# First expert weights as the stationary operand, loaded tile by tile from DRAM

## The chip, the cores and the metric

The kernel runs on one core of a Trainium2 chip. Times are device microseconds of one launch. Three runs of the kernel before took 886.35, 894.93 and 897.02 us; their median, 894.93, is the time before. The profile is of a further execution, of 883.17 us, whose span from the first to the last instruction is 881.4 us.

## The reference

`x` has 16 x 256 tokens of 128 numbers. The network adds a mixture of experts, an attention and the same mixture again:

```python
x = x + 0.5 * _L0_ffn_ref(_layernorm(x), ...)
x = x + _L0_attn_ref(_layernorm(x), ...)
x = x + 0.5 * _L0_ffn_ref(_layernorm(x), ...)
```

In the mixture each token goes to 4 of 32 experts:

```python
t = _rmsnorm(x, norm_scale)
g = t @ gate_w.T + gate_b
vals, idx = jax.lax.top_k(gf, K)
w = jax.nn.softmax(vals, axis=-1)
h1 = jnp.einsum('th,efh->tef', tf, w1) + b1
h = _swiglu(h1)          # min(glu, 7) * sigmoid(1.702 * glu) * (clip(lin, -7, 7) + 1)
hw = h * combine[:, :, None]
out = jnp.einsum('tef,ehf->th', hw, w2) + combine @ b2
return x + out
```

The reference computes all experts and weights most with zero; the kernel computes the chosen ones only. All numbers are float32.

## The kernel before

**Groups and runs.** The 4096 tokens are two groups of four blocks of 512 tokens. Each group passes the mixture twice, so there are four expert runs, called f0, f1 (first mixture, group 0 and 1) and l0, l1 (second mixture). In names of tiles the page shows `_f` for f0 and f1, `_l` for l0 and l1. `route` chooses the experts of a block; `dispatch` sorts the rows of a group by expert, makes the table `at_w` (which expert each tile of rows belongs to) and scatters the rows into the DRAM buffer `xs` with indirect DMAs from POOL. `experts` computes one run and writes its rows into the DRAM buffer `ys`. `combined` gathers them back (`gt`), weights and adds them (`pu`).

**A quad.** Rows come in tiles of 125 rows of one expert; four tiles are a quad, and a run has 28 quads. For quad q, `experts` calls three functions:

- `enter` loads the quad's rows `xq` from `xs` (two DMAs on SP, L658), transposes the four tiles on PE into `pxT` (L650), and copies that on ACT to `xT` (L652).
- `first` reads the four experts from `at_w` into PE's registers (L631), multiplies each tile of `xT`, which is the stationary operand, by 256 columns of its expert's weights in `w_sb` (L671: `ph`, two tiles to a PSUM tile), and forms the gated product `a`: Silu on ACT (L675), clipping into `lin` on DVE (L676), both for two tiles at a time, and one scalar_tensor_tensor on DVE for all four (L681, called STT in what follows). Tokens lie on the partitions.
- `second` transposes `a` on PE into `phT` (L650), copies that on ACT to `hT` (L652), multiplies by the second weights, also in `w_sb` (L688: `po`), copies `po` to `yq` on ACT (L693) and writes `yq` to `ys` (two DMAs on SP, L695).

The loop calls `enter(q + 1)`, `first(q)` and `second(q - 1)`, and then `beside()`, which advances the background work of another group by a few steps:

```python
beside = [enter(1), middle(0), middle(1), leave(0)]
steps = [2, 5, 5, 2]
```

So f0 has the routing of group 1 beside it, f1 and l0 have combination, attention and routing of a group, and l1 has the last combination of group 0. `leave(1)` follows alone.

**Order.** The program is recorded in this order and a scheduler then places each engine's instructions in one order of that engine, by its own estimate of when they can run. On the chip an engine follows its list. SP's list holds all DMAs but the indirect ones; a DMA there also waits until the DMA eight places earlier on the list has landed, since eight semaphores are used in turn.

**Weights.** `w_sb` holds for each of the 32 experts 256 columns of first weights and 128 of second weights, loaded at the start. `fold_experts` multiplies the norm's scale and the first bias into the first weights in place: for every two experts two matmuls (L285, L286: `pw`) and one DVE instruction (L289). Attention's weights are folded in `fold_attention`. `xs` is cleared at the start by DMAs from a tile of zeros.

Of the kernel before, what the change touches and what calls it, by code (L numbers as in the profile page):

```python
# [10 lines left out]
F32 = mybir.dt.float32  # L11
# [3 lines left out]
AF = mybir.ActivationFunctionType  # L15
ALU = mybir.AluOpType
AX = mybir.AxisListType
PE = mybir.EngineType.PE
DVE = mybir.EngineType.DVE
PSUM = bass.MemoryType.PSUM  # L20
DRAM = bass.MemoryType.DRAM

P = 128
NJ = 4
# [4 lines left out]
NE = 32  # L29
# [1 line left out]
NH = 16  # L31
HD = 8
KVW = P + NH
EW = 3 * P


RB = 5
# [3 lines left out]
RT = BT * RB  # L41
# [5 lines left out]
LIMIT = 7.0  # L47
ALPHA = 1.702
# [7 lines left out]
def kernel(  # L56
# [22 lines left out]
    nc = tc.nc  # L79
# [9 lines left out]
    wpool = ctx.enter_context(tc.tile_pool(name="weights", bufs=1))  # L89
# [151 lines left out]
        )  # L241


    w_sb = wpool.tile([P, NE, EW], F32, tag="w_sb", name="w_sb")
    for c in range(NE // 8):
        s = slice(c * 8, (c + 1) * 8)
        nc.sync.dma_start(w_sb[:, s, 0 : 2 * P], w1[:, s].rearrange("h e t f -> h e (t f)"))
        nc.sync.dma_start(w_sb[:, s, 2 * P : EW], w2[:, s])
    w_flat = w_sb.rearrange("p e c -> p (e c)")

    cleared(0)

# [60 lines left out]
    pairs = []  # L313
# [8 lines left out]
        pairs.append(pr)  # L322

    def fold_experts():
        for c in range(NE // 2):
            folded(
                w_sb[:, 2 * c : 2 * c + 2, 0 : 2 * P], b1_w.rearrange("p r f -> p (r f)"),
                pairs[c // (NE // 4)][:, c % (NE // 4), :], f"w{c}",
            )
        nc.vector.tensor_scalar(b2_sb, b2_sb, ALPHA, None, ALU.mult)  # L330

# [176 lines left out]
    def dispatch(st):  # L508

        name, n = st.name, st.n  # L510
# [51 lines left out]
        st.at_w = small.tile([P, NT], I32, tag="at_w", name=f"at_w_{name}")  # L562
        ex = small.tile([P, NT], F32, tag="ex", name=f"ex_{name}")
        nc.vector.tensor_scalar(ex, pex[:, 0:NT], float(NE - 1), None, ALU.min)
        nc.vector.tensor_scalar(st.at_w, ex, float(EW), None, ALU.mult)
        yield
        sc = []
        for b in range(GB):
# [58 lines left out]
                yield  # L627
        scattered[name] = sc

    def loaded(tab, q, engine, top):  # L630
        _, vals = nc.values_load_multi_w_load_instructions(  # L631
            tab[0:1, q * NJ : (q + 1) * NJ], engines=[engine],
            min_val=0, max_val=top, skip_runtime_bounds_check_because="made on the chip from at most NE - 1",
        )
        return vals

    def experts(st, beside):
# [4 lines left out]
        xT, hw, off = {}, {}, {}  # L642

        parts = slice(0, RT // 16 * 16), slice(RT // 16 * 16, RT)

        def turned(src, name):

            pt = ps_t.tile([P, NJ, P], F32, tag="tp", name=f"p{name}")
            for t in range(NJ):
                nc.tensor.transpose(pt[:, t, 0:RT], src[:, t, :], ident[:RT, :RT])  # L650
            dst = ep.tile([P, NJ, RT], F32, tag=name[0:2], name=name)
            nc.scalar.copy(dst, pt[:, :, 0:RT])  # L652
            return dst

        def enter(q):
            xq = ep.tile([RT, NJ, P], F32, tag="xq", name=f"xq_{name}_{q}", bufs=2)
            for rows in parts:
                nc.sync.dma_start(xq[rows], xs_q[q].rearrange("j m h -> m j h")[rows])  # L658
            xT[q] = turned(xq, f"xT_{name}_{q}")

        def first(q):
            off[q] = loaded(st.at_w, q, PE, (NE - 1) * EW)
            a = ep.tile([RT, NJ, P], F32, tag="a", name=f"a_{name}_{q}")
            lin = ep.tile([RT, NJ, P], F32, tag="lin", name=f"lin_{name}_{q}")
            x_q = xT.pop(q)
            for c in range(2):
                ph = ps_h.tile([P, 2, 2 * P], F32, tag="ph", name=f"ph_{name}_{q}_{c}")
                ts = slice(2 * c, 2 * c + 2)
                for s in range(2):
                    t = 2 * c + s  # L670
                    nc.tensor.matmul(  # L671
                        ph[:RT, s, :], x_q[:, t, :],
                        w_flat[:, bass.ds(off[q][t], 2 * P)], start=True, stop=True,
                    )
                nc.scalar.activation(a[:, ts, :], ph[:RT, :, 0:P], AF.Silu, scale=ALPHA)  # L675
                nc.vector.tensor_scalar(  # L676
                    lin[:, ts, :], ph[:RT, :, P : 2 * P], LIMIT + 1.0, 1.0 - LIMIT,
                    ALU.min, ALU.max,
                )

            nc.vector.scalar_tensor_tensor(a, a, SILU_LIMIT, lin, ALU.min, ALU.mult)  # L681
            hw[q] = a

        def second(q):
            hT = turned(hw.pop(q), f"hT_{name}_{q}")
            po = ps_o.tile([P, NJ, P], F32, tag="po", name=f"po_{name}_{q}")
            for t in range(NJ):
                nc.tensor.matmul(  # L688
                    po[:RT, t, :], hT[:, t, :],
                    w_flat[:, bass.ds(off[q][t] + 2 * P, P)], start=True, stop=True,  # L690
                )
            yq = ep.tile([RT, NJ, P], F32, tag="yq", name=f"yq_{name}_{q}", bufs=2)
            nc.scalar.copy(yq, po[:RT])  # L693
            for rows in parts:
                nc.sync.dma_start(ys_q[q].rearrange("j m h -> m j h")[rows], yq[rows])  # L695
# [296 lines left out]
```

## Time and profile before

| | |
|---|---|
| median of three runs | 894.93 us (886.35 to 897.02) |
| profiled execution | 883.17 us, span 881.4 us |
| granted TensorE clock, mean | 0.967 |
| busy: PE, DVE, ACT, POOL | 87%, 61%, 55%, 18% of the span |
| DMA moved | 134.22 MB, mean 152 GB/s |
| HBM read, written | 62.88 MB, 70.27 MB |

A line of the timeline has the start, the length, the engine, the line of the kernel, the operation and its tiles (out<-in), and in square brackets the idle time before it and what ended it. A PE record of a float32 matmul comes twice, since it is made in two passes; a transpose comes once. A record's length reaches past the start of the next, since PE is a pipeline; so spacing of starts, and not length, tells what one costs. `x8` joins eight neighbours. `SPq` is SP's queue. A line of a group has busy time, mean length of one in ns, idle time of the engine before them and what ended it.

### The profile page before, as it was taken

What the parts mean: (1) busy time and instruction counts of PE and PEld (TensorE: products, weight loads), DVE (VectorE), ACT (ScalarE), POOL (GpSimd) and SP (SyncE); (2) the same over time, 40 slices, a digit from 0 to 9 for tenths busy, and PEclk for the clock granted to TensorE, in tenths of its full rate; (3) what the DMA queues carried; (4) which work ended last, traced back from release to release, by engine and by line L of the source; (5) the groups of instructions that cost most, each with busy time, mean ns of one, the idle gap of its engine ahead of it and who ended that gap; (6) DMA issues with size and microseconds to landing.
All of it is one profiled execution on the core that took longest, in us unless ns stands there. A gap on an engine that the chain in (4) does not pass through costs nothing.

```text
span 881.4 us, 16078 instructions
## 1 busy us (share of the span) xinstructions
PE 766.5 (87%) x5018; PEld 648.3 (74%) x5033; DVE 538.3 (61%) x1903; ACT 486.6 (55%) x964; POOL 155.6 (18%) x211
## 2 busy tenths in 40 slices
PE   4789689899979898989998989888898899999566
PEld 2336578799868787877887878777797788787456
DVE  6676875675554876758854777676874344433232
ACT  1412288755556588697453687968655345455100
POOL 4003400022212201000434112000242321000232
PEclk9999989999999999999999999999999999999688
DMA  8996535455545434224556344223465665553442
GB/s 259 342 355 238 178 116 156 110 161 176 181 135 148 139 92 138 70 71 135 172 179 180 100 136 132 81 83 87 150 201 163 181 175 160 140 143 93 116 133 84
DMA packets 155505, 134.22 MB, mean 152 GB/s; under 512 B 10528, under 2 KB 143136, under 8 KB 155424
## 3 DMA queue, kind: packets, MB, share of 16 engines
q1 hardware_dynamic: 145184, 91.24, 36.3%
q0 software_dynamic: 10240, 41.95, 14.7%
q8 instruction: 44, 0.72, 0.3%
q14 instruction: 37, 0.30, 0.1%
HBM read 62.88 MB, written 70.27 MB: 151 GB/s over the span
## 4 chain that ended last, share of the span: by engine, by line
PE 56%; ACT 12%; DVE 6%; DMA 5%; issue 4%; POOL 1%; SPq 0%; POOLq 0%; ACTq 0%; DVEq 0%
PE ph_l L671 9%; PE ph_f L671 8%; PE po_l L688 6%; PE po_f L688 5%; PE pu_l L749 4%; PE pu_f L749 4%; PE p_l L610 3%; ACT hT_l L652 2%; PE phT_l L650 2%; PE phT_f L650 2%; ACT L675 2%; ACT hT_f L652 2%; PE p_f L610 2%; PE pxT_f L650 1%; PE pxT_l L650 1%
## 5 line engine op out<-in xcount | busy, mean ns | idle before, releaser
L671 PE MATMUL ph_f<-w_sb,xT_f 128*125 x448 | 114.4, 388 | 3.6 <-DVE lin_f L676 2.9
L671 PE MATMUL ph_l<-w_sb,xT_l 128*125 x448 | 111.2, 383 | 0.9 <-PE pq L270 0.3
L676 DVE TENSOR_SCALAR lin_l<-ph_l 125x256 f32<-125x256 f32 x112 | 46.1, 421 | 85.9 <-ACT a_l L675 85.6
L671 PEld LDWEIGHTS ph_f<-w_sb,xT_f 128*125 128x125 f32 x448 | 78.4, 190 | 15.1 <-DVE lin_f L676 3.6
L671 PEld LDWEIGHTS ph_l<-w_sb,xT_l 128*125 128x125 f32 x448 | 78.1, 187 | 13.8 <-issue 3.2
L676 DVE TENSOR_SCALAR lin_f<-ph_f 125x256 f32<-125x256 f32 x112 | 45.7, 420 | 53.9 <-ACT a_f L675 53.7
L688 PE MATMUL po_f<-w_sb,hT_f 128*125 x448 | 64.1, 286 | 12.9 <-ACT hT_f L652 12.2
L688 PE MATMUL po_l<-w_sb,hT_l 128*125 x448 | 64.3, 287 | 11.9 <-ACT hT_l L652 11.1
L688 PEld LDWEIGHTS po_l<-w_sb,hT_l 128*125 128x125 f32 x448 | 54.5, 190 | 23.0 <-ACT hT_l L652 21.8
L688 PEld LDWEIGHTS po_f<-w_sb,hT_f 128*125 128x125 f32 x448 | 54.4, 190 | 22.8 <-ACT hT_f L652 21.6
L749 PE MATMUL pu_l<-gt_l,u_l 128*128 128x128 f32 x320 | 52.5, 311 | 16.2 <-DMA gt_l<-ys,row_l 12.1
L749 PEld LDWEIGHTS pu_l<-gt_l,u_l 128*128 128x128 f32 x320 | 48.6, 225 | 20.6 <-issue 14.8
L693 ACT COPY yq_l<-po_l 125x512 f32<-125x512 f32 x56 | 32.8, 586 | 55.4 <-PE po_l L688 50.0
L675 ACT ACTIVATE a_l<-ph_l 125x256 f32<-125x256 f32 x112 | 42.0, 385 | 35.8 <-PE ph_l L671 35.1
L693 ACT COPY yq_f<-po_f 125x512 f32<-125x512 f32 x56 | 32.7, 585 | 47.5 <-PE po_f L688 39.7
L719 POOL DMA_INDIRECT gt_f<-ys,row_f x32 | 31.6, 986 | 151.2 <-PE pu_f L749 94.3
L675 ACT ACTIVATE a_f<-ph_f 125x256 f32<-125x256 f32 x112 | 41.4, 384 | 29.8 <-PE ph_f L671 29.0
L719 POOL DMA_INDIRECT gt_l<-ys,row_l x32 | 31.0, 970 | 144.4 <-PE pu_l L749 63.4
L675 ACT ACT_TABLE_LOAD x41 | 52.6, 1283 | 2.8 <-PE ph_l L671 1.0
L749 PE MATMUL pu_f<-gt_f,u_f 128*128 128x128 f32 x320 | 45.8, 287 | 5.7 <-DMA gt_f<-ys,row_f 5.7
L616 POOL DMA_INDIRECT xs<-s_l,row_l x32 | 33.5, 1046 | 92.1 <-ACT s_l L614 61.9
L616 POOL DMA_INDIRECT xs<-s_f,row_f x32 | 31.8, 994 | 90.2 <-DVE o_f L602 69.2
(325 smaller groups left out, 1702.5 us busy)
## 6 DMA issues: line engine op xcount, KB each, us to landing
xs<-zero SPq DMA_DIRECT2D x2, 7000.0 KB
xq_f<-xs SPq DMA_DIRECT2D x56, 224.0 KB
ys<-yq_f SPq DMA_DIRECT2D x56, 224.0 KB
xq_l<-xs SPq DMA_DIRECT2D x56, 224.0 KB
ys<-yq_l SPq DMA_DIRECT2D x56, 224.0 KB
w_sb<-in_w_dram SPq DMA_DIRECT2D x4, 1024.0 KB
x<-in_x_dram SPq DMA_DIRECT2D x8, 256.0 KB
w_sb<-in_w_dram SPq DMA_DIRECT2D x4, 512.0 KB
```

Source lines behind the costliest of these rows:

```text
L610: nc.tensor.matmul(p0[:, r, :] if r < 4 else p1[:, 0:P], o[:, r, :], k.tn[:, t, :], start=True, stop=True,)
L616: ins = nc.gpsimd.indirect_dma_start(out=xs[st.g][:, :], out_offset=bass.IndirectOffsetOnAxis(ap=st.row[:, 1, j : j + 1], axis=0), in_=s.r ...
L650: nc.tensor.transpose(pt[:, t, 0:RT], src[:, t, :], ident[:RT, :RT])
L652: nc.scalar.copy(dst, pt[:, :, 0:RT])
L671: nc.tensor.matmul(ph[:RT, s, :], x_q[:, t, :], w_flat[:, bass.ds(off[q][t], 2 * P)], start=True, stop=True,)
L675: nc.scalar.activation(a[:, ts, :], ph[:RT, :, 0:P], AF.Silu, scale=ALPHA)
L676: nc.vector.tensor_scalar(lin[:, ts, :], ph[:RT, :, P : 2 * P], LIMIT + 1.0, 1.0 - LIMIT, ALU.min, ALU.max,)
L688: nc.tensor.matmul(po[:RT, t, :], hT[:, t, :], w_flat[:, bass.ds(off[q][t] + 2 * P, P)], start=True, stop=True,)
L693: nc.scalar.copy(yq, po[:RT])
L719: nc.gpsimd.indirect_dma_start(out=gt.rearrange("p r h -> p (r h)"), out_offset=None, in_=ys[st.g][:, :], in_offset=bass.IndirectOffsetOnA ...
L749: nc.tensor.matmul(pu[:, t, :], u[:, r, s, :], got[t][:, r, :], start=(r == 0), stop=False)
```

## The change

The first matmul's operands change places: the weights of 128 columns are stationary and the 125 rows of `xT` stream, so `ph` comes out with the hidden index on the partitions, and the gated product can be the second matmul's stationary operand as it is. The second transposition and its copy are gone. There are twice as many first matmuls, of 125 columns each.

The first weights no longer stay in SBUF. After the fold they are written to a DRAM buffer `w1_d`, and `enter` loads for each tile its expert's 128 x 256 weights from there, four DMAs a quad on SP whose DRAM address comes from a register; SP reads `at_w` for that itself. The tiles are six buffers deep. The same six buffers serve the fold: six of its eight parts of four experts are loaded at the start, and parts 6 and 7 take over a buffer once part 0 and part 1 have been written to `w1_d`. The second weights stay in SBUF, in `w2_sb`, and PE reads `at_w` in `second`.

```diff
-    w_sb = wpool.tile([P, NE, EW], F32, tag="w_sb", name="w_sb")
+    WE = 4
+    w1_d = dram.tile([NE, P, 2 * P], F32, tag="w1_d", name="w1_d")
+    w1_rows = w1_d.rearrange("e h c -> (e h) c")
+    w2_sb = wpool.tile([P, NE, P], F32, tag="w2_sb", name="w2_sb")
+    w2_flat = w2_sb.rearrange("p e c -> p (e c)")
+
+    def w1_tile(name):
+        return ep.tile([P, WE, 2 * P], F32, tag="w1", name=name, bufs=6)
+
+    w1_parts = {}
+
+    def load_w1(c):
+        w1_parts[c] = w1_tile(f"w1_{c}")
+        s = slice(c * WE, (c + 1) * WE)
+        nc.sync.dma_start(w1_parts[c], w1[:, s].rearrange("h e t f -> h e (t f)"))
+
+    for c in range(6):
+        load_w1(c)
     for c in range(NE // 8):
         s = slice(c * 8, (c + 1) * 8)
-        nc.sync.dma_start(w_sb[:, s, 0 : 2 * P], w1[:, s].rearrange("h e t f -> h e (t f)"))
-        nc.sync.dma_start(w_sb[:, s, 2 * P : EW], w2[:, s])
-    w_flat = w_sb.rearrange("p e c -> p (e c)")
+        nc.sync.dma_start(w2_sb[:, s], w2[:, s])
...
     def fold_experts():
-        for c in range(NE // 2):
-            folded(
-                w_sb[:, 2 * c : 2 * c + 2, 0 : 2 * P], b1_w.rearrange("p r f -> p (r f)"),
-                pairs[c // (NE // 4)][:, c % (NE // 4), :], f"w{c}",
+        for c in range(NE // WE):
+            if c not in w1_parts:
+                load_w1(c)
+            part = w1_parts.pop(c)
+            for i in range(WE // 2):
+                d = c * WE // 2 + i
+                folded(
+                    part[:, 2 * i : 2 * i + 2, :], b1_w.rearrange("p r f -> p (r f)"),
+                    pairs[d // (NE // 4)][:, d % (NE // 4), :], f"w{d}",
+                )
+            nc.sync.dma_start(
+                w1_d[c * WE : (c + 1) * WE].rearrange("e h c -> h e c"), part
             )
...
-        def turned(src, name):
-
-            pt = ps_t.tile([P, NJ, P], F32, tag="tp", name=f"p{name}")
-            for t in range(NJ):
-                nc.tensor.transpose(pt[:, t, 0:RT], src[:, t, :], ident[:RT, :RT])
-            dst = ep.tile([P, NJ, RT], F32, tag=name[0:2], name=name)
-            nc.scalar.copy(dst, pt[:, :, 0:RT])
-            return dst
...
         def enter(q):
             xq = ep.tile([RT, NJ, P], F32, tag="xq", name=f"xq_{name}_{q}", bufs=2)
             for rows in parts:
                 nc.sync.dma_start(xq[rows], xs_q[q].rearrange("j m h -> m j h")[rows])
-            xT[q] = turned(xq, f"xT_{name}_{q}")
+            w1_q[q] = w1_tile(f"w1_{name}_{q}")
+            at = loaded(st.at_w, q, SP)
+            for t in range(NJ):
+                nc.sync.dma_start(w1_q[q][:, t, :], w1_rows[bass.ds(at[t], P), :])
+            pt = ps_t.tile([P, NJ, P], F32, tag="tp", name=f"pxT_{name}_{q}")
+            for t in range(NJ):
+                nc.tensor.transpose(pt[:, t, 0:RT], xq[:, t, :], ident[:RT, :RT])
+            xT[q] = ep.tile([P, NJ, RT], F32, tag="xT", name=f"xT_{name}_{q}")
+            nc.scalar.copy(xT[q], pt[:, :, 0:RT])
 
         def first(q):
-            off[q] = loaded(st.at_w, q, PE, (NE - 1) * EW)
-            a = ep.tile([RT, NJ, P], F32, tag="a", name=f"a_{name}_{q}")
-            lin = ep.tile([RT, NJ, P], F32, tag="lin", name=f"lin_{name}_{q}")
-            x_q = xT.pop(q)
+
+            a = ep.tile([P, NJ, RT], F32, tag="a", name=f"a_{name}_{q}")
+            lin = ep.tile([P, NJ, RT], F32, tag="lin", name=f"lin_{name}_{q}")
+            x_q, w_q = xT.pop(q), w1_q.pop(q)
             for c in range(2):
-                ph = ps_h.tile([P, 2, 2 * P], F32, tag="ph", name=f"ph_{name}_{q}_{c}")
+                ph = ps_h.tile([P, 2, 2, P], F32, tag="ph", name=f"ph_{name}_{q}_{c}")
                 ts = slice(2 * c, 2 * c + 2)
                 for s in range(2):
                     t = 2 * c + s
-                    nc.tensor.matmul(
-                        ph[:RT, s, :], x_q[:, t, :],
-                        w_flat[:, bass.ds(off[q][t], 2 * P)], start=True, stop=True,
-                    )
-                nc.scalar.activation(a[:, ts, :], ph[:RT, :, 0:P], AF.Silu, scale=ALPHA)
+                    for part in range(2):
+                        nc.tensor.matmul(
+                            ph[:, part, s, 0:RT], w_q[:, t, part * P : (part + 1) * P],
+                            x_q[:, t, :], start=True, stop=True,
+                        )
+                nc.scalar.activation(a[:, ts, :], ph[:, 0, :, 0:RT], AF.Silu, scale=ALPHA)
                 nc.vector.tensor_scalar(
-                    lin[:, ts, :], ph[:RT, :, P : 2 * P], LIMIT + 1.0, 1.0 - LIMIT,
+                    lin[:, ts, :], ph[:, 1, :, 0:RT], LIMIT + 1.0, 1.0 - LIMIT,
                     ALU.min, ALU.max,
                 )
...
         def second(q):
-            hT = turned(hw.pop(q), f"hT_{name}_{q}")
+            at = loaded(st.at_w, q, PE)
+            hT = hw.pop(q)
             po = ps_o.tile([P, NJ, P], F32, tag="po", name=f"po_{name}_{q}")
             for t in range(NJ):
                 nc.tensor.matmul(
-                    po[:RT, t, :], hT[:, t, :],
-                    w_flat[:, bass.ds(off[q][t] + 2 * P, P)], start=True, stop=True,
+                    po[:RT, t, :], hT[:, t, :], w2_flat[:, bass.ds(at[t], P)],
+                    start=True, stop=True,
                 )
```

More of the change, by code (lines that the diff above doesn't have):

```diff
@@ L18 @@
 PE = mybir.EngineType.PE
-DVE = mybir.EngineType.DVE
+SP = mybir.EngineType.SP
 PSUM = bass.MemoryType.PSUM
@@ L33 @@
 KVW = P + NH
-EW = 3 * P
 RB = 5
@@ L564, in dispatch @@
         nc.vector.tensor_scalar(ex, pex[:, 0:NT], float(NE - 1), None, ALU.min)
-        nc.vector.tensor_scalar(st.at_w, ex, float(EW), None, ALU.mult)
+        nc.vector.tensor_scalar(st.at_w, ex, float(P), None, ALU.mult)
         yield
@@ L628, in dispatch, with loaded @@
         scattered[name] = sc
-    def loaded(tab, q, engine, top):
+    def loaded(tab, q, engine):
         _, vals = nc.values_load_multi_w_load_instructions(
             tab[0:1, q * NJ : (q + 1) * NJ], engines=[engine],
-            min_val=0, max_val=top, skip_runtime_bounds_check_because="made on the chip from at most NE - 1",
+            min_val=0, max_val=(NE - 1) * P, skip_runtime_bounds_check_because="made on the chip from at most NE - 1",
         )
@@ L641, in experts @@
         ys_q = ys[g].rearrange("(q j n) (r h) -> q j (n r) h", j=NJ, n=BT, r=RB)
-        xT, hw, off = {}, {}, {}
+        xT, w1_q, hw = {}, {}, {}
         parts = slice(0, RT // 16 * 16), slice(RT // 16 * 16, RT)
-        def turned(src, name):
-            pt = ps_t.tile([P, NJ, P], F32, tag="tp", name=f"p{name}")
-            for t in range(NJ):
-                nc.tensor.transpose(pt[:, t, 0:RT], src[:, t, :], ident[:RT, :RT])
-            dst = ep.tile([P, NJ, RT], F32, tag=name[0:2], name=name)
-            nc.scalar.copy(dst, pt[:, :, 0:RT])
-            return dst
         def enter(q):
```

## The prediction, on record before the changed kernel ran

> **What bounds the kernel.** I read the page's engine shares first, then the chain that ended last, then the four expert runs as windows, then one quad in the timeline.
>
> ```profile
> PE 766.5 (87%) x5018; PEld 648.3 (74%) x5033; DVE 538.3 (61%) x1903; ACT 486.6 (55%) x964; POOL 155.6 (18%) x211
> ...
> PE 56%; ACT 12%; DVE 6%; DMA 5%; issue 4%; POOL 1%; SPq 0%; POOLq 0%; ACTq 0%; DVEq 0%
> ```
>
> PE is busiest and holds most of the chain. The windows run from the first yq copy of a run to its last (f0, f1, l0, l1); columns are length, busy time of PE, PEld, DVE, ACT, POOL, clock, DMA share, GB/s.
>
> ```profile
> 124.70:255.30 130.60, 121.58 (x875) 108.49 (x875) 79.14 (x256) 87.09 (x177) 15.96 (x19) 1.00 0.51 149
> 269.40:466.00 196.60, 178.93 (x1273) 156.73 (x1276) 139.99 (x503) 139.83 (x276) 31.24 (x35) 0.99 0.43 125
> 479.80:675.70 195.90, 178.48 (x1271) 156.85 (x1274) 140.02 (x503) 139.72 (x275) 30.79 (x32) 0.99 0.43 126
> 686.50:820.50 134.00, 124.77 (x830) 108.52 (x833) 56.97 (x124) 66.54 (x136) 16.13 (x16) 1.00 0.54 143
> ```
>
> The four make 657 of 881.4 us and PE is busy 91 to 93% of each, so experts are bound by what PE does and waits for. The shortest quad, in l1 with no background work beside it:
>
> ```profile
> 788.26 1.14 PE L688 MATMUL po_l<-w_sb,hT_l 128*125 x8 [0.29 <-ACT hT_l L652]
> ...
> 789.24 1.92 PE L671 MATMUL ph_l<-w_sb,xT_l 128*125 x8
> ...
> 790.09 0.82 SPq L695 DMA_DIRECT2D ys<-yq_l  x2
> ...
> 790.99 0.59 PE L650 MATMUL phT_l<-ident,a_l 125*128 125x125 f32 x4
> 791.19 0.39 ACT L675 ACTIVATE a_l<-ph_l 125x256 f32<-125x256 f32 x1 [0.43 <-PE ph_l L671]
> ...
> 791.42 0.59 PE L650 MATMUL pxT_l<-ident,xq_l 125*128 125x125 f32 x4
> 791.61 0.42 DVE L676 TENSOR_SCALAR lin_l<-ph_l 125x256 f32<-125x256 f32 x1 [0.39 <-ACT a_l L675]
> 791.67 0.58 ACT L652 COPY hT_l<-phT_l 128x500 f32<-128x500 f32 x1
> 792.04 0.81 SPq L658 DMA_DIRECT2D xq_l<-xs  x2
> 792.07 0.69 DVE L681 SCALAR_TENSOR_TENSOR a_l<-a_l,lin_l 125x512 f32<-125x512 f32 x1
> 792.14 0.58 ACT L652 COPY xT_l<-pxT_l 128x500 f32<-128x500 f32 x1
> 792.30 1.14 PE L688 MATMUL po_l<-w_sb,hT_l 128*125 x8 [0.30 <-ACT hT_l L652]
> ```
>
> A quad takes 792.30 - 788.26 = 4.04 us. Starts of neighbouring records lie 216 ns apart for 256 moving columns, 109 for 128, 106 for the transposes' 125. PE work: pxT 4 x 0.106, ph 8 x 0.216, phT 4 x 0.106, po 8 x 0.109, in all 3.45. The rest is the wait for hT. The phT of quad q-1 stands behind ph of q, so the gate chain (ACT, lin, STT) has a quad to hide in.
>
> **Removed.** phT (0.42 on PE a quad) and its copy on ACT (0.58). All 112 quads lose both; no phT stands in the changed program. The wait for hT goes:
>
> ```profile
> L688 PE MATMUL po_l<-w_sb,hT_l 128*125 x448 | 64.3, 287 | 11.9 <-ACT hT_l L652 11.1
> L688 PE MATMUL po_f<-w_sb,hT_f 128*125 x448 | 64.1, 286 | 12.9 <-ACT hT_f L652 12.2
> ```
>
> 24.8 us, some 6 a run. The ACT time (112 x 0.58 = 65 us) is under PE work and brings nothing itself.
>
> **Changed on PE.** ph becomes sixteen passes of 125 columns on 128-column weights; the nearest row is the transposes' own form (125 columns, 128 weights), so 16 x 0.106 = 1.70 for 1.73. PE work is 2.99 a quad, 0.46 less: 12.8 us a run. Were the pass the 109 of po, 1.74: 1.4 us a run worse.
>
> **Moved: the order on PE.** This decides the sum. The scheduler's lists for the changed program can be read before it runs; they hold no times. In them po of q stands behind ph of the *same* q in f0 and l1. The tail of l1 reads pxT22, ph22, po22, pxT23, ph23, po23; ACT has a22, a22, yq22, xT23. In f1 and l0 it is mostly ph of q, po of q-1, with background between. Two chains then lie open:
> - Gate: last ph slot ends 790.99; ACT, lin and STT end at 792.76; po could start at 792.8: 1.8 us less PE work listed between. With po's and ph's operands now f-major the three sizes are the same (250, 250, 500 elements).
> - xT: slot end of pxT at 791.84, copy 0.27 later and 0.58 long, ph 0.1 later: 0.9. With yq ahead of it on ACT, 1.5 from po's end.
>
> So a quad in that tail takes 1.70 + 1.8 + 0.87 + 1.5 = 5.9 us against 4.04. Adding up, quad by quad, what the listing leaves uncovered of 1.8 and 0.85, with each listed PE instruction at its spacing: f0 28, f1 4, l0 2, l1 27 (30 with yq's place). In l1 the gate stays open by 1.6, 1.8, 1.8, 1.4, 0.9 and six times 1.8 in quads 17 to 27, and by 0.5 in all earlier ones together, since there background or the next pxT stands between; xT adds 0.8 in each of the last six and 3 elsewhere. In f0 quads 4 to 8 leave 1.2 to 1.8 each (xT 0.8 in three), the later ones 0 to 1.4, as enter(1)'s few PE instructions cover them. The trace has no such order; nothing says that these waits vanish, but background work which itself waits may cover some (low end half, 30), and DVE's background queue lengthens the gate in f0: in the listing up to 36 DVE instructions stand ahead of one lin. I add 8 there, 20 at the high end.
>
> **Added: 4 loads a quad, a table load and 4 address steps on SP.** A table load is 0.33 us (on PE today), an address step 0.05. Issues run 0.30 to 0.47; one with a register address is not in the trace, so 0.30 (the cheapest row) to 1.0 (twice the dearest usual one). Nearest are the x and xq rows, so 0.45: SP has 0.82 + 0.81 + 0.33 + 4 x 0.5 = 4.0 us a quad, under the 4.5 to 7 of the new quads, so I take no cost, and at 0.30 no gain, as SP does not bind; behind the loads wait ys of q-2 and xq of q+1 only. The order puts w1 of q behind ys of q-3 or so: 0.8 + 0.8 + 2.3 issue and some 2 to land, against two quads. A ninth DMA on SP waits for the landing of the first of eight, a quad earlier: hidden too.
>
> ```profile
> q1 hardware_dynamic: 145184, 91.24, 36.3%
> q0 software_dynamic: 10240, 41.95, 14.7%
> ```
>
> Packets cost 0.363 x 16 x 881.4 / 145184 = 35 ns at 628 bytes and 202 at 4 KB: 54 by a line for 1 KB (estimate). 512 packets on 16 engines are 1.7 us a quad, 193 in all: share 0.51 to 0.73. gt lands in 4.0 to 4.4 us today; I add 4 us over its 64 (0 to 20).
>
> **A rule against it.** The Trainium skill, "DMA: Bandwidth & Descriptors" (Anatomy of one DMA; Bandwidth), fits 2.0 us + bytes/436e3 for a DMA of GpSimd and advises 1 MiB each. Four of 128 KB one after another would be 9.2 us a quad: f0 and l1 at 258 us each instead of 131 and 134, +251. But the trace shows overlap: the chain that ended last has the pair of xq DMAs of one quad, 250 KB, at 2.47 us, where the rule gives 2.5 for the larger alone and 4.6 for both in series. I take the row: overlapped.
>
> **Added: the fold.** 12 of 16 folds stay among the dispatch; w1 parts 6 and 7 must wait for a buffer, so part 0 is written out, 6 loaded, folded, written, and only then w1_f0_0 is read. On SP these stand behind xr of block 3, whose DVE step ran at 98.95; with four folds fewer before it I take 92. Four writes (2 MB, 7 us), two loads (4), 8 fold matmuls (8), write and w1 loads (8): first ph near 120 against 113.57. +6 (0 to +12).
>
> **Sum**, against the profiled execution (span 881.4, 883.17 in all):
> - f0: -12.8 - 6 + 28 + 8 = +17
> - f1: -12.8 - 6 + 4 = -15; l0: -12.8 - 6 + 2 = -17. Background chains fill part of the hole: DVE and ACT are 71% busy there. I give back a quarter: +8.
> - l1: -12.8 - 6 + 30 = +11
> - gt +4, start +6.
>
> +14, 1.6%: 897 for that execution (883.17 + 14). The median of the runs is 894.93, 1.3% above it; I put +14 on the median: **909**.
>
> **Rivals.**
> 1. *SP becomes the bound* (slower). Place: SP's order in f0 and l1. Price: if a register-addressed issue takes 1.0 instead of 0.45, SP has 6.2 a quad and f0 and l1 take 174 each, +83 in place of my +28; with the other terms +69: 964. It decides from 0.65 an issue, where SP reaches the 4.9 of the mean quad. For: eight issues instead of four, and in-order waits. Against: issues in the trace keep to 0.30 to 0.47.
> 2. *The stalls are covered* (faster). Background waits overlap half of the 64 us of open chains, DVE's queue adds nothing and the start is free: 14 - 32 - 8 - 6 = -32: 863. For: DVE and ACT shed work. Against: l1's last eleven quads have no background at all.
> 3. *The clock gate.* "TensorE: Matmul & The Clock Gate" (Why this matters for your kernels): gaps over about 3 us take PE to half clock. The trace agrees:
>
> ```profile
> 107.19 1.25 PE L270 MATMUL pt_f<-ident,tn_f 128*128 128x128 f32 x4 [4.52 <-DVE tn_f L434]
> ...
> 113.57 3.63 PE L671 MATMUL ph_f<-w_sb,xT_f 128*125 x8
> ```
>
> Behind a gap of 4.52, ph takes 3.63 for 1.92. My gaps are 1.8 and 1.5, and 0.29 to 1.44 kept the clock at 1.00. If they close it, 16 bare quads cost 3.0 more: +48, 957.
>
> **Chances.** Forecast 0.57 (own range 892 to 926), rival 1 and other slow transfers 0.24, rival 3 0.05, rival 2 0.14. By 2% (17.9 us), about what a measurement can tell: the forecast's share splits 0.35 same, 0.22 slower; rival 2 gives 0.10 faster, 0.04 same; 1 and 3 give 0.25 slower, 0.04 same. With every unknown at its dear end (ph passes 6, DVE 12, gt 16, start 6 more) the forecast's sum is +54, 949; the range, 876 to 955, takes that in and part of rivals 1 and 2.
>
> **What would show it.** ph rows near 106 ns apart; po waiting for DVE a (STT) about 36 us in f runs and 20 in l runs; f1 and l0 about 10 us shorter, f0 and l1 longer; l1's last quads near 5.9; the ACT copies of L652 halved; first ph near 120. Wrong if po waits for nothing, if ph waits for w1 DMAs (rival 1), or if PEclk in f0 or l1 falls under 0.9.

## The result, and the profile after

The changed kernel takes **940.69 us** (median of four runs, 935.63 to 951.78) against 890.64 for the kernel before in the same session: **1.058 times** as long, with a 95% interval of 1.046 to 1.071. The forecast was 909; the change costs 50 us where the working found 14. The profiled execution shown here is the longest of the four (951.78 us, span 950.1); a second one of the same program has a span of 947.2 and the same picture. Ratios here are of the faster executions alone, while both profiles of the changed kernel are of slower ones, so their spans are 66 to 69 us above the one before where the ratio makes 52: windows tell where the time went, ratios how much it was.

The first view again is the engines' shares, with PE's clock by slices and the two data queues:

```profile
PE 775.9 (82%) x5481; PEld 675.5 (71%) x5481; DVE 532.7 (56%) x1903; ACT 419.1 (44%) x845; POOL 155.5 (16%) x211
...
PEclk9999859779999799998999999999998999998677
...
q1 hardware_dynamic: 207328, 154.19, 56.3%
q0 software_dynamic: 10240, 41.95, 14.0%
```

PE is busy for 9 us more than before although each quad gives it less to do, and its share fell from 87 to 82%: it works part of the time at half clock (the 5, 7, 6 of the clock row) and waits more. The table of the four expert runs, from the first yq copy of a run to its last, has the columns of the prediction's table:

```profile
150.90:307.40 156.50, 125.09 (x970) 116.94 (x970) 86.82 (x296) 74.86 (x154) 15.90 (x19) 0.91 0.71 208
327.30:517.30 190.00, 171.48 (x1368) 159.63 (x1367) 138.27 (x508) 121.46 (x246) 32.33 (x34) 0.96 0.69 200
534.20:719.70 185.50, 167.46 (x1371) 156.26 (x1369) 137.40 (x504) 122.60 (x246) 30.27 (x32) 0.98 0.72 208
732.00:891.30 159.30, 123.14 (x940) 112.83 (x938) 58.30 (x127) 51.00 (x108) 15.91 (x16) 0.96 0.73 204
```

Against the windows of before: the start (up to the first yq) +26.2 us, f0 +25.9, f1 -6.6, l0 -10.4, l1 +25.3, the gaps between the runs +10.4, the end -2.1; together the 68.7 us between the spans. The signs are those of the prediction; the start, f0 and l1 are too large, and the gaps were not in it.

One bare quad at the end of l1, and the next:

```profile
851.16 2.05 PE L694 MATMUL ph_l<-xT_l,w_l 128*128 128x125 f32 x16 [0.77 <-ACT xT_l L681]
...
854.94 1.11 PE L712 MATMUL po_l<-w_sb,a_l 128*125 x8 [1.73 <-DVE a_l L704]
...
855.88 0.59 PE L679 MATMUL pxT_l<-ident,xq_l 125*128 125x125 f32 x4
...
857.25 3.68 PE L694 MATMUL ph_l<-xT_l,w_l 128*128 128x125 f32 x16 [0.77 <-ACT xT_l L681]
...
862.65 1.11 PE L712 MATMUL po_l<-w_sb,a_l 128*125 x8 [1.73 <-DVE a_l L704]
```

The order is ph, po, pxT of one quad and then ph of the next. From po to po the second quad takes 862.65 - 854.94 = 7.71 us, the one before it 6.1. Both have the same two waits: 1.73 us for the gate chain and 0.77 for the xT copy. What differs is ph itself, 2.05 us in one and 3.68 in the other: PE's clock is halved there, though no gap is longer than 1.73 us.

The groups show who waits for whom in the whole execution:

```profile
L694 PE MATMUL ph_f<-xT_f,w_f 128*128 128x125 f32 x896 | 131.2, 296 | 9.5 <-ACT xT_f L681 4.8
...
L712 PE MATMUL po_f<-w_sb,a_f 128*125 x448 | 68.3, 291 | 25.5 <-DVE a_f L704 22.0
...
L712 PE MATMUL po_l<-w_sb,a_l 128*125 x448 | 63.2, 277 | 18.5 <-DVE a_l L704 17.3
...
L679 PE MATMUL pxT_l<-ident,xq_l 125*128 125x125 f32 x224 | 36.4, 282 | 18.5 <-DMA xq_l<-xs 18.5
```

po's wait for hT has become a wait for a, 39 us in all. pxT, whose l group waited 0.1 us in the kernel before, now waits 18.5 us for its rows. That row points at SP. The queue view of SP tells what SP itself waits for (us, times, longest). Before:

```profile
SPq L695 <- ACT yq_l L693: 126.0, 41, 8.9
SPq L695 <- ACT yq_f L693: 111.7, 36, 9.3
SPq L658 <- PE pxT_f L650: 81.9, 37, 9.9
SPq L658 <- PE pxT_l L650: 77.0, 38, 9.3
```

After:

```profile
SPq L719 <- ACT yq_l L717: 59.3, 32, 5.4
SPq L719 <- ACT yq_f L717: 56.3, 24, 9.2
...
SPq L471 <- DVE xr_f L467: 43.3, 2, 32.7
...
SPq L672 <- PE pxT_l L679: 7.9, 6, 2.1
```

Before, SP stood for 159 us with a load of xq in hand and waited for a free buffer: it ran ahead of PE, and that wait was its slack. It stood 238 us more for yq, and still PE waited only 1.7 us for xq: to stand at a result costs nothing while the list has a lead. After, pxT_l is waited for 7.9 us and pxT_f 3.8. The slack is gone. The wait for yq is shorter than before, 116 us, but what stands behind it on the list no longer has a lead. Of the 116, 5.0 us lie in f0 and 24.4 in l1. PE itself waits there mostly for the gate chain: 20.7 us for a and 2.0 for xq in f0, 16.4 and 8.8 in l1.

Added up over the records in the four windows, SP's own issuing (table loads included) rose from 1.9 to 4.2 us a quad.

The late start, in the timeline:

```profile
104.40 0.34 SPq L471 DMA_DIRECT2D xr_f<-xr_f  x1
104.79 3.66 SPq L350 DMA_DIRECT2D w_d<-w  x4
108.56 1.72 SPq L258 DMA_DIRECT2D w<-in_w_dram  x2
117.03 2.07 PE L300 MATMUL pw_w<-w,less 128*128 128x512 f32 x2 [7.37 <-DMA w<-in_w_dram]
...
133.94 0.38 SPq L350 DMA_DIRECT2D w_d<-w  x1
...
137.31 4.84 SPq L676 DMA_DIRECT2D w_f<-w_d  x8
...
142.33 1.06 PE L694 MATMUL ph_f<-xT_f,w_f 128*128 128x125 f32 x4
```

The write of w1 parts stands behind xr of block 3 on SP's list, which waits 32.7 us for DVE. Only at 108.56 are parts 6 and 7 asked for; PE stands still for 7.37 us, then folds them at half clock (2.07 us for two records where the kernel before has 1.08), and the first ph comes at 142.33, not 113.57.

### The profile page after: what moved, and what is told of

It is laid out like the page before. It is cut to its first block, busy times and chain, and to the rows that moved or that the text cites. A ratio compares the mean times of both kernels' runs of the same rounds, so it can differ in the third digit from the quotient of the medians.

```text
span 950.1 us, 17992 instructions
## 1 busy us (share of the span) xinstructions
PE 775.9 (82%) x5481; PEld 675.5 (71%) x5481; DVE 532.7 (56%) x1903; ACT 419.1 (44%) x845; POOL 155.5 (16%) x211
## 5 line engine op out<-in xcount | busy, mean ns | idle before, releaser
L694 PE MATMUL ph_f<-xT_f,w_f 128*128 128x125 f32 x896 | 131.2, 296 | 9.5 <-ACT xT_f L681 4.8
L694 PE MATMUL ph_l<-xT_l,w_l 128*128 128x125 f32 x896 | 129.2, 295 | 10.1 <-ACT xT_l L681 6.7
L694 PEld LDWEIGHTS ph_l<-xT_l,w_l 128*128 128x128 f32 x896 | 120.0, 210 | 16.0 <-ACT xT_l L681 10.0
L694 PEld LDWEIGHTS ph_f<-xT_f,w_f 128*128 128x128 f32 x896 | 120.9, 211 | 13.5 <-ACT xT_f L681 6.5
L699 DVE TENSOR_SCALAR lin_l<-ph_l 128x250 f32<-128x250 f32 x112 | 46.1, 414 | 114.3 <-ACT a_l L698 114.0
L712 PE MATMUL po_f<-w_sb,a_f 128*125 x448 | 68.3, 291 | 25.5 <-DVE a_f L704 22.0
L699 DVE TENSOR_SCALAR lin_f<-ph_f 128x250 f32<-128x250 f32 x112 | 45.3, 413 | 77.7 <-ACT a_f L698 77.2
L712 PEld LDWEIGHTS po_f<-w_sb,a_f 128*125 128x125 f32 x448 | 59.2, 199 | 31.1 <-issue 11.9
L712 PE MATMUL po_l<-w_sb,a_l 128*125 x448 | 63.2, 277 | 18.5 <-DVE a_l L704 17.3
L712 PEld LDWEIGHTS po_l<-w_sb,a_l 128*125 128x125 f32 x448 | 55.1, 188 | 23.3 <-issue 18.1
L773 PE MATMUL pu_l<-gt_l,u_l 128*128 128x128 f32 x320 | 50.4, 309 | 14.8 <-DMA gt_l<-ys,row_l 10.6
L679 PE MATMUL pxT_l<-ident,xq_l 125*128 125x125 f32 x224 | 36.4, 282 | 18.5 <-DMA xq_l<-xs 18.5
```

Of the source, the lines that this page charges most:

```text
L679: nc.tensor.transpose(pt[:, t, 0:RT], xq[:, t, :], ident[:RT, :RT])
L694: nc.tensor.matmul(ph[:, part, s, 0:RT], w_q[:, t, part * P : (part + 1) * P], x_q[:, t, :], start=True, stop=True,)
L699: nc.vector.tensor_scalar(lin[:, ts, :], ph[:, 1, :, 0:RT], LIMIT + 1.0, 1.0 - LIMIT, ALU.min, ALU.max,)
L712: nc.tensor.matmul(po[:RT, t, :], hT[:, t, :], w2_flat[:, bass.ds(at[t], P)], start=True, stop=True,)
L773: nc.tensor.matmul(pu[:, t, :], u[:, r, s, :], got[t][:, r, :], start=(r == 0), stop=False)
```

## The experiments

**Theory O** (order and clock): in f0 and l1 po of q stands behind ph of the same q, which opens the gate chain, and the idle time halves the clock. **Theory L** (loads): the four loads a quad cost more than "hidden", by SP's list or by their transfers. A third question is the start. Times are medians; ratios are against the kernel before on the same chip; windows come from one profiled execution of each.

| kernel | us | ratio (95%) | first yq | f0 | f1 | l0 | l1 |
|---|---|---|---|---|---|---|---|
| before (first profile) | 894.93 | | 124.7 | 130.6 | 196.6 | 195.9 | 134.0 |
| changed, again | 945.24 | 1.060 (1.049 to 1.070) | 154.4 | 153.1 | 190.3 | 188.0 | 154.7 |
| resident, fixed experts | 833.85 | 0.946 (0.937 to 0.955) | 120.3 | 115.1 | 188.0 | 187.6 | 110.9 |
| tied order | 965.5 | 1.093 (1.087 to 1.098) | 140.0 | 172.8 | 195.7 | 187.0 | 156.3 |
| eight buffers | 935.68 | | 126.3 | 163.4 | 190.0 | 186.0 | 158.3 |
| tied, a quarter of the rows | 1060.69 | 1.195 (1.182 to 1.209) | 155.1 | 196.1 | 219.9 | 206.7 | 177.0 |
| tied, ys on ACT | 890.44 | 0.998 (0.993 to 1.003) | 148.2 | 136.3 | 186.5 | 190.2 | 126.5 |
| resident, late order in l1 | 873.95 | 0.987 (0.975 to 1.000) | 132.9 | 115.2 | 187.8 | 186.7 | 146.1 |
| the same with filler | 864.52 | 0.977 (0.961 to 0.992) | 132.8 | 115.3 | 187.9 | 188.5 | 142.3 |
| ys on ACT alone | 894.74 | 1.008 (1.003 to 1.013) | 140.6 | 139.7 | 201.6 | 198.5 | 127.9 |
| tied, ys on ACT, eight | 895.5 | 1.003 (0.999 to 1.007) | 131.3 | 146.3 | 189.9 | 189.0 | 121.2 |
| the same, two quads ahead | 886.61 | 0.999 (0.995 to 1.002) | 128.3 | 147.2 | 183.5 | 188.9 | 130.0 |
| before with ys on ACT | 898.6 | 1.013 (1.001 to 1.024) | 127.1 | 130.8 | 202.5 | 203.0 | 138.2 |

### The changed kernel again

> The changed kernel once more, for a profile that stands beside those of the experiments. Theory O (order and clock): the last bare quads of l1 take 6.1 us where PE keeps its clock and some 7.7 where it is at half clock; f0 and l1 last 22 to 28 us longer than before, f1 and l0 7 to 10 us less. Theory L (loads): ph waits for w loads, or SP has no free time, and all quads of f0 and l1 lie near one length. Time near 940 us.

It repeats: +5.9%. In its l1 the last quads are 6.1, 6.1, 6.1, 6.1, 6.1 and 7.7; in the first profile 7.7, 6.1, 7.7, 6.1 and 7.6. So the half clock comes and goes between executions of one program, and with it some us of l1 (154.7 against 159.3).

### The swap alone: resident weights

```diff
-            w1_q[q] = w1_tile(f"w1_{name}_{q}")
-            at = loaded(st.at_w, q, SP)
-            for t in range(NJ):
-                nc.sync.dma_start(w1_q[q][:, t, :], w1_rows[bass.ds(at[t], P), :])
...
-                            ph[:, part, s, 0:RT], w_q[:, t, part * P : (part + 1) * P],
+                            ph[:, part, s, 0:RT], w1_sb[:, (q * NJ + t) % NE, part * P : (part + 1) * P],
```

> The swap of operands alone: all first weights stay in SBUF and there are no loads from DRAM and no table on SP. Each tile's first weights are those of a fixed expert by the tile's place instead of the table's expert; this part of the computation is changed. In the program's list po of q-1 stands behind ph of q in nearly all quads. If the swap does what it was credited with (12.8 us less PE work and 6 us of waits a run): f0 and l1 about 113, f1 and l0 about 181, first ph near 114; 820 us. If the swap itself costs (twice as many ph passes, weight loads that do not hide): f0 and l1 at 130 or more, 880 us or more.

Whether the table's own experts could be taken from SBUF as the stationary operand was not tried. The swap does what it was credited with in f0 and l1 (115.1 and 110.9 for 113), and less in f1 and l0 (188 for 181). The part of l1 without background, in the timeline:

```profile
752.34 1.95 PE L684 MATMUL ph_l<-xT_l,w_sb 128*128 128x125 f32 x16
754.13 1.04 PE L702 MATMUL po_l<-w_sb,a_l 128*125 x8
755.00 0.59 PE L669 MATMUL pxT_l<-ident,xq_l 125*128 125x125 f32 x4
...
755.43 1.95 PE L684 MATMUL ph_l<-xT_l,w_sb 128*128 128x125 f32 x16
```

A quad is 755.43 - 752.34 = 3.09 us, where the prediction's PE work was 2.99, and PE waits for nothing. With the loads, SP's table reads and the way of the folded weights through DRAM removed, po of q-1 stands behind ph of q again in nearly all quads. So the loads and what belongs to them cost all that was lost and more: 122 us between the spans, 825.1 and 947.2, and 100 us by the ratios, 0.946 and 1.060.

### The order tied by hand

```diff
+                        if t == 0 and part == 0:
+                            behind(last_ph[q], turn.get(q + 1))   # ph of q behind pxT of q + 1
...
+                if t == 0:
+                    behind(m, last_ph.get(q + 1))                 # po of q behind ph of q + 1
```

`behind` adds an edge that fixes the place on PE's list and no wait.

> The changed kernel with the order on PE tied by hand: pxT of q+1, then ph of q, then po of q-1, with no other edit. Theory O: the gate chain has a quad to hide in again and PE has no idle stretches, so f0 falls from 157 to about 130, l1 from 159 to about 125, po's wait for a goes from 44 us to under 10 in all, and the clock of both runs is over 0.97; the start keeps its 26 us. Sum about 890 us. Theory L (a bare quad is bounded by SP's 4.0 us of issues or by transfers, at a DMA share of 0.73 over 5.6 us, which is 4.1 us of all 16 engines a quad): the waits only change their names, f0 and l1 stay over 150, ph waits for w; 930 us or more.

Theory O fails as stated: the kernel gets slower still, 965.5. po no longer waits for a; the wait has moved to the next thing that is late:

```profile
L689 PE MATMUL pxT_f<-ident,xq_f 125*128 125x125 f32 x224 | 40.7, 306 | 44.1 <-DMA xq_f<-xs 44.1
L689 PE MATMUL pxT_l<-ident,xq_l 125*128 125x125 f32 x224 | 39.1, 295 | 40.2 <-DMA xq_l<-xs 39.2
...
L724 PE MATMUL po_l<-w_sb,a_l 128*125 x448 | 61.9, 276 | 2.7 <-ACT yq_l L731 1.0
```

The timeline of its l1 shows why xq is late:

```profile
867.15 0.90 SPq L682 DMA_DIRECT2D xq_l<-xs  x2
...
871.22 0.59 ACT L731 COPY yq_l<-po_l 125x512 f32<-125x512 f32 x1 [0.79 <-PE po_l L724]
...
871.83 0.82 SPq L733 DMA_DIRECT2D ys<-yq_l  x2
...
873.81 3.14 SPq L686 DMA_DIRECT2D w_l<-w_d  x4
...
877.05 0.38 SPq L682 DMA_DIRECT2D xq_l<-xs  x1
...
881.20 1.06 PE L689 MATMUL pxT_l<-ident,xq_l 125*128 125x125 f32 x4 [5.68 <-DMA xq_l<-xs]
```

From 868.05 to 871.83 SP stands before the ys write, 3.8 us, as the write waits for yq; only then come the four w loads, and only then the next xq. PE needs xq to reach the po that makes the next yq. SP waits for PE and PE for SP.

### ys on another queue, with the tied order and alone

```diff
-                nc.sync.dma_start(ys_q[q].rearrange("j m h -> m j h")[rows], yq[rows])
+                nc.scalar.dma_start(ys_q[q].rearrange("j m h -> m j h")[rows], yq[rows])
```

> The tied order with the two ys writes of a quad issued on ACT's queue, just behind the yq copy they wait for, in place of SP's. SP loses 0.85 us of issues a quad and all its waits for yq (135 us in the tied kernel); ACT gains the issues. Theory S: pxT's wait for xq falls from 83 us to under 30, f0 and l1 under 135, the time 900 us or less. Theory T: xq stays late, the time within 2% of the tied kernel's 965 us.

890.44: 75 us less than with the tied order alone, in f0 and l1 mostly (172.8 to 136.3, 156.3 to 126.5). xq's wait falls from 83 to 31 us.

> The changed kernel with one edit: the two ys writes of a quad go out on ACT's queue. No order is tied; in the program's list po of q-1 then stands behind ph of q again in l1's bare quads, by the scheduler's own choice. If SP's list is the root of both (the late xq and the order of po), this alone does what order and queue did together: f0 about 136, l1 about 127, 890 us. If the tied order was needed as well: over 910 us.

The one edit, without any tied order, gives 894.74, a ratio of 1.008 for 1.060. That is some 46 us, nearly all that the change had cost (the medians, of two chips, differ by 50.5). The scheduler's own list then has ph of q ahead of po of q-1 in the bare quads again. So one edit mends both the order on PE and the late xq. It fits this that the scheduler had put po early because its estimate had ph late behind SP's full list; its estimates were not seen, so that is not shown. The windows, f0 and l1:

```profile
140.60:280.30 139.70, 122.07 (x975) 116.51 (x977) 85.45 (x295) 74.00 (x155) 15.90 (x19) 0.93 0.80 235
...
706.70:834.60 127.90, 110.97 (x933) 105.16 (x937) 52.75 (x116) 45.58 (x107) 15.79 (x16) 1.00 0.85 241
```

Against the changed kernel's second profile the span is 54 us shorter: start 14, f0 13, l1 27. f1 and l0 grow by 11 each, and the gaps ahead of them shrink by as much. The 14 us of the start arise before any ys is written: xr of block 3 goes out at 93.71 instead of 107.23. The tied kernel, with ys on SP, has it at 93.54 and its first yq at 140.0. So they belong to another order of the program there, and 40 of the 54 us are what ys costs in f0 and l1.

> The kernel before with the one edit of the two ys writes on ACT's queue. If the writes' place matters only where SP's list is full (in the changed kernel): SP has 1.7 us of issues a quad here and runs ahead, xq waits for a free buffer and never PE for xq, so the time stays within 1% of the kernel before. If the edit is a gain of its own (ys lands sooner, SP asks for xq sooner): 870 us or less, and the 50 us it brought the changed kernel are not a repair of what the change broke.

In the kernel before, the same edit gives a ratio of 1.013 (1.001 to 1.024), a little outside the expected 1% and no gain. It repairs what the loads broke.

### A quarter of the bytes

```diff
-                nc.sync.dma_start(w1_q[q][:, t, :], w1_rows[bass.ds(at[t], P), :])
+                nc.sync.dma_start(w1_q[q][:KT, t, :], w1_rows[bass.ds(at[t], KT), :])   # KT = 32
```

> The tied order with a quarter of the bytes: each load takes the first 32 of the 128 rows of a tile's first weights, and the first matmul sums over those 32 rows only; this part of the computation is left out. SP issues as many DMAs, in the same places, and PE makes as many passes of the same columns. Theory T (the loads' transfers fill the DMA engines and make xq late): pxT's wait for xq falls from 83 us to under 25 and f0 and l1 come near 115 to 125, the time near 880 us. Theory S (SP's list in order: 4.2 us of issues and table load a quad, and xq behind ys, which waits for yq): the waits stay within a fifth, f0 and l1 over 150, the time over 945 us.

Neither: xq's waits fell to 46 us, between the two, and yet the kernel became 95 us slower. The mean clock is 0.801; in all four runs it is 0.775 to 0.801, where the tied order had 0.880 to 0.912. In its l1 a quad reads:

```profile
971.63 3.77 PE L705 MATMUL ph_l<-xT_l,w_l 32*128 32x125 f32 x16
...
975.33 2.07 PE L725 MATMUL po_l<-w_sb,a_l 128*125 x8
...
977.19 1.04 PE L690 MATMUL pxT_l<-ident,xq_l 125*128 125x125 f32 x4
978.16 3.77 PE L705 MATMUL ph_l<-xT_l,w_l 32*128 32x125 f32 x16
```

This stretch begins behind a wait of 3.66 us for xq. From there PE has no gap for 13.3 us and yet stays at half clock. It is not a single case. In all traces of this case the clock changes only on a grid of 3.413 us. From 120 us on this kernel has 70 such windows in which PE is busy for 90% or more at half clock and the clock stays at half behind them, and 5 at full clock behind which it falls; the tied kernel has none of either. Both make the same passes, so it is the 32 rows in use instead of 128 that do not hold the clock up. The question transfers against SP is not settled by this run; the move of ys, which leaves every byte in place, shows that SP's list was most of what made xq late.

### The late order and the clock, without any loads

The resident kernel, with pxT, ph, po of one quad after the other in l1's quads 17 to 27:

```diff
+                if t == 0 and name == "l1" and q > 17:
+                    behind(m, last_po[q - 1])
...
+            if name == "l1" and q >= 17:
...
+                    first(q)
+                    second(q)
+                    if q + 1 < NQ:
+                        enter(q + 1)
```

> Resident first weights and no loads, each tile with a fixed expert by its place in place of the table's, but in l1's quads 17 to 27 the order on PE is tied as the changed kernel has it: pxT, ph and po of one quad, then the next. Theory O (order and clock): these quads take 6.1 and 7.7 us in turns as in the changed kernel, where they take 3.1 without the tie; l1 goes from 111 to 144 to 152 us, which is the changed kernel's 155 but for some loads. Theory L (late loads are what opens the gaps): they take under 5 us without any loads.

l1 goes from 110.9 to 146.1. (Only l1 is compared: the start of this execution is 12.6 us later by a fold at half clock, which the edit doesn't touch.) Its last quads are 7.5, 6.1, 7.5, 6.1, 7.5 and 6.1, as in the changed kernel:

```profile
777.55 1.11 PE L714 MATMUL po_l<-w_sb,a_l 128*125 x8 [1.73 <-DVE a_l L706]
778.50 0.59 PE L679 MATMUL pxT_l<-ident,xq_l 125*128 125x125 f32 x4
...
779.86 2.05 PE L696 MATMUL ph_l<-xT_l,w_sb 128*128 128x125 f32 x16 [0.77 <-ACT xT_l L683]
```

The waits are the same 1.73 and 0.77 to the hundredth. So in the tail of l1 the order accounts for the quads' length, and no load needs to be late there.

```diff
+            if name == "l1" and q >= 17:
+                for _ in range(12):
+                    nc.tensor.transpose(po[:RT, 0, 0:RT], ident[:RT, :RT], ident[:RT, :RT])
```

> The kernel before this one in the list, with twelve transposes of a constant into po's tile in each of those eleven quads, five ahead of ph and seven behind it, where PE waits; po's own matmuls write over them. They need 1.3 us of the 2.5 us that PE stands idle in a quad. If the half clock comes from PE's idle share: no quad is over 6.4 us, all near 6.1, l1 6 to 9 us shorter than without them. If the slow quads have another cause: they stay at 7.7 in turns, or all quads grow by the 1.3 us.

```profile
774.64 2.05 PE L696 MATMUL ph_l<-xT_l,w_sb 128*128 128x125 f32 x16 [0.77 <-ACT xT_l L683]
...
776.52 1.47 PE L715 MATMUL po_l<-ident 125*125 125x125 f32 x12
```

All quads of the tail are 6.1 to 6.4, none 7.5, and l1 is 3.8 us shorter with more work in it, where 6 to 9 were expected. In the quad shown all twelve run in the gate's gap, of which 0.42 us is left. PE stands idle for 2.5 us of 6.1 without them and for 1.2 with them.

One profile of each would not prove much: in the second profile of the changed kernel five quads with the same waits kept the clock. The grid of the clock tells more. Two of its windows of 3.41 us in the late order without filler, with PE's busy time first:

```profile
795.83:799.24 3.41, 1.54 (x12) 1.34 (x12) 1.10 (x2) 0.91 (x3) 0.00 (x0) 1.00 0.09 24
802.66:806.07 3.41, 1.69 (x16) 1.53 (x14) 1.10 (x2) 0.47 (x2) 0.00 (x0) 1.00 0.00 0
```

Behind the first, with PE busy for 45%, the clock is at half for a window; behind the second, with 49%, it stays full, though this one holds a whole wait of 1.72 us and the first only parts of two. In the tails of l1 of five profiles (the changed kernel twice, eight buffers, late order, filler) the clock fell 13 times, always behind windows with PE busy for 40 to 49%, and stayed full behind 67 others, of 49% and more; the filler's have 63% and more. So it is the sum of the waits in such a window that counts there and not the longest one, and where the grid falls decides which quad is slow. Elsewhere in the executions the clock also fell behind busier windows, up to 77%, so the busy share is not the whole account.

### The fold's buffers

```diff
-        return ep.tile([P, WE, 2 * P], F32, tag="w1", name=name, bufs=6)
+        return ep.tile([P, WE, 2 * P], F32, tag="w1", name=name, bufs=8)
...
-    for c in range(6):
+    for c in range(8):
```

> The changed kernel with eight buffers for the w1 tiles in place of six, all eight parts loaded at the start, so no part of the fold waits for a buffer. If the buffers are the cause of the late start: the first ph comes near 125 us instead of 142 (4 MB still have to be written before the first load), time about 17 us less, some 924 us. If the xr wait on SP and PE's half clock in the fold are the cause: first ph stays over 138 and the time within 5 us of the changed kernel.

The first ph comes at 116.25 instead of 142.33, even earlier than expected, so the two missing buffers and what they wait for are the late start. But f0 then takes 163.4 instead of 156.5 or 153.1 and gives 7 to 10 us back. The medians differ by 9.6 us; with four runs each that is no firm number.

### The repairs together

> Tied order, ys on ACT's queue, and eight w1 buffers with all parts of the fold loaded at the start. If the three repairs add up: first yq near 125 instead of 148 us and 15 to 20 us less than the kernel with the first two (890), about 872 us, 1.5% under the kernel before. If an earlier start only meets the busier DMA engines of f0 (share 0.83): f0 grows by what the start gives and the time stays at 885 us or more.

> The same with rows and weights of a quad asked for two quads ahead instead of one (three xq and three xT buffers). If the rest of the loss against resident weights (f0 +21, l1 +16 us) is latency: f0 near 120 and l1 near 113, about 845 to 855 us. If it is the DMA engines' capacity (share 0.83 and 0.84 in these runs) or SP's issue time: within 1% of the kernel before it in the list.

The first yq comes at 131.3 instead of 148.2, f0 takes 10 us more, and the time is 895.5: no gain over 890.44. The expected 872 was wrong; the repairs don't add up. Asking two quads ahead ends at 886.61, 0.4% less by the ratios and level with the kernel before the change (0.999). It did not bring f0 near 120 or l1 near 113, so asking earlier is not what was missing. With resident weights DMA shares were 0.58 and 0.63 in f0 and l1; with loads and ys on ACT they are 0.79 to 0.86. In l1 of the kernel with ys alone moved, 0.85 x 127.9 / 27 = 4.0 us of all 16 DMA engines a quad stands against PE's 3.1. Whether transfers or SP's issuing bound it was not separated. In f0 of that kernel, 24.6 us above the resident one, the loss is in two halves: PE waits 11.6 us more, and it is busy for 13.1 us more, at a clock of 0.93 instead of 1.00. To leave ys on SP and put the loads on another queue was not tried.

## Why the prediction was off, step by step

The forecast was +14, the change cost +50. 940.69 is outside the forecast's own range, 892 to 926. That it lies in the wide one, 876 to 955, is partly luck: its upper part came from dear values of the ph passes, DVE, gt and the start, +54 in all, and of these only the start turned out dear. The rest of the excess is in the gaps between the runs and in f0 and l1, whose loss hangs on SP's list.

- **Removed work and PE's quad: right.** 2.99 us of PE work a quad; 3.09 with nothing to wait for. The resident kernel is 15.5 and 23.1 us shorter than before in f0 and l1, where 18.8 each was claimed, but only 8.6 and 8.3 in f1 and l0, where the claim less the give-back was 14.8.
- **The order on PE: right, its size in part.** po waits 17.3 us for a in the l runs, where 20 was named, but 22.0 in the f runs, where 36 was. A bare quad takes 6.1; 5.9 was worked out. But the order was taken as a thing of its own: moving two writes off SP's list turned it back, and tying it by hand alone made the kernel slower.
- **"I take no cost" for SP: the step that failed.** The size was right, 4.2 us a quad for the 4.0 of the sum. A table load was dearer on SP than PE's 0.33 (17.1 us for 25 in f0, 0.68) and an issue cheaper than 0.45 (38.0 us for 99, 0.38). What failed is the test: 4.0 under 4.5 to 7 is the test for a queue that runs freely. SP's list also stands still at ys until yq exists, 3.8 us in the timeline of the tied order. "Behind the loads wait ys of q-2 and xq of q+1 only" named the right instructions and left out that ys waits in its turn. Taking ys off the list is worth 40 us of span in f0 and l1 (13 and 27). In the changed kernel most of that shows as PE's waits for a, 37 us there, which the prediction had priced as the order of PE; so the number missed less than the mechanism. f0 and l1 of the second profile are 82 us above the resident kernel, where the order terms had 66. Moving ys takes two things away from SP, 0.85 us of issues a quad and the waits (116 us in the whole execution). The runs don't part the two; in f0, where SP stood only 5.0 us for yq, the waits can't be much of it directly.
- **Rival 1** had the right place and the wrong trigger. It was to decide from 0.65 us an issue (its own sum gives 0.69); it decided at 0.38. The 0.30 to 0.47 that it read from the trace are medians: in the l1 of before the ys issues take 0.48 on average.
- **Start +6: it was +26 at the first yq,** the largest single miss. The order of its steps was right (xr, writes, loads, fold, writes), the terms were not. xr of block 3 was put at 92 and came at 104.4; the last of the fold came at half clock; the first loads of the run wait for the last write. Two more buffers, for which SBUF had room, take it away.
- **The clock: called unlikely, and it happened**, with gaps of 1.73 and 0.77. The reading "0.29 to 1.44 kept the clock" compared single gaps; in the tails of l1 their sum in a window of the grid counts. The Trainium skill, "TensorE: Matmul & The Clock Gate" (Part 1: The HAM clock gate), says that the clock follows how busy PE has been in a free-running window of 3413 ns. The traces agree: their clock changes on that grid, and in the tails of l1 it fell behind windows of 40 to 49%. The prediction cited only the rule for long gaps. What the clock costs in l1 is small: 3.8 us in the resident kernel.
- **DMA share 0.51 to 0.73: right** (0.70 over the span, 0.71 in f0, 0.73 in l1). The loads overlap, as the row was preferred to the rule for: f0 and l1 are 157 and 159 us, far from the 258 that four loads in series would have made. **gt +4:** PE's waits for gt are 14.7 us, and were 17.8; nothing was added.
- **The sum.** Against the windows of the first profile the start misses by 20 us (26 for 6), l1 by 14 (25 for 11), the gaps by 10 (no term), f0 by 9 (26 for 17), f1 and l0 by 7 together. By cause, the prediction had -75 for the swap, +8 given back and +82 for order (72), gt (4) and start (6). Measured in spans: the swap -56 (881.4 to 825.1), which is 11 less than claimed, and the loads +122 (825.1 to 947.2), 40 more. By the ratios it is -48 and +100. Of the 122, 40 are ys on SP's list in f0 and l1 and 14 the other order of the start; 68 remain when ys is moved: start 20, f0 25, l1 17, the middle runs with their gaps 6.

## What to carry to other kernels

A DMA queue is a list in order. Before you add issues to it, look at what it waits for: waits for free buffers are slack and may be filled. A wait for a result of the same loop costs nothing while the list has a lead (238 us of it before the change), and holds up all loads behind it once the lead is used up. Put writes of results on a queue that doesn't carry the next loads, or show that the list keeps its lead. And when a scheduler's order looks bad, ask whether a late input lies behind it before you force another.

## What was not expected of the hardware

- Matmuls with 32 rows in use ran PE without a gap at half clock (ph 3.77 us for 16 passes, clock 0.801); those with 128 rows ran 1.95 at full clock. At full clock, 16 passes with 32 rows took 2.04. Keeping PE busy isn't enough.
- Two short waits, 1.73 and 0.77 us in each 6.1, can halve the clock: in one profile in every other quad, in another of the same program in one of six.
- A table load into registers took 0.68 us on SP, 0.33 on PE.
- Moving two writes of a quad from SP's queue to ACT's was worth some 46 us by the ratios, with not a byte less moved. The Trainium skill's front page, "Trainium Kernel Development and Optimization" (Key Constraints), says that issuing from several engines only saves the sequencer's issue time, since all queues share 16 DMA engines. Here the writes' wait for yq leaves the list as well, and the timeline of the tied order has 3.8 us of such standing for 0.82 of issuing.
